# A graph-attention layer and an expert layer in one kernel: the first group's look-ups, the split of src and the tables of pairs take other places in the order

## The chip, the cores and the metric

The kernel runs on one core of one Trainium2 chip. The metric is the device time of one execution in microseconds (us). A core has five engines that work side by side and hand over by semaphores: TensorE (PE, matrix products and transposes), VectorE (DVE), ScalarE (ACT), GpSimd (POOL) and SyncE (SP, which here only issues transfers). Each engine takes its own instructions strictly in the order in which the program lists them, so an instruction that waits holds up all that stand behind it on its engine.

## What is computed

```python
xn  = layernorm(x)                                   # x: 6250 x 256
xt  = (xn @ weight).reshape(6250, 4, 64)
row, col = src, dst                                  # only the first 6250 edges reach the output
a   = softmax(leaky_relu(al(xt[row]) + ar(xt[col])), axis=heads)   # al, ar: products with attn_l, attn_r
tmp = sum over heads of a[n, h] * xt[col[n], h, :]
x   = x + tmp, the same 64 columns for each of the 4 heads
t   = layernorm(x)
logits = t @ router_w.T;  top 2 of 8 experts, two weights
x   = x + t + sum over the two experts of weight * (gelu(t @ w1[e] + b1[e]) @ w2[e] + b2[e])
```

## The kernel before

Rows lie on 128 partitions in 49 tiles; five groups of 10, 10, 9, 10 and 10 tiles are worked one after the other. The order on every engine is the order of the program text (manual schedule): no planner moves anything. The first 190 us or so have these stages.

**Setup (lines 186 to 365).** SP issues the loads of dst, src and x, ACT those of the weights. PE, DVE and ACT fold the weights (`raw`, `own`, `terms`, `turned`, `twice`). Lines 337 to 358 are the split of src on DVE: eleven small instructions turn each index into a partition number `hi` and a column `low`. Line 360 transposes `hi` on PE into the PSUM tile `pe`, line 362 copies it to `high_b` on DVE, and lines 364 and 365 send it through DRAM back to all partitions as `high_1`.

**The source phase (lines 679 to 696).** Thirteen blocks `k` of up to four tiles of x. For each, PE transposes the *next* block (`turn`, line 247), then multiplies this one (`own_terms`, line 434); ACT copies the result to `own_T` (line 439), and PE turns it back one block later (`back`, line 448). Beside this DVE computes the row statistics of each of four parts (`source_statistics`, lines 418 and 420) and ends each part (`source_end`, lines 457 to 467), which yields `al_sb`. The dictionary `fillers` hangs other work on single blocks: `weights_columns` behind block 1, `pair_tables` behind block 2, the tables `low_0` (line 664) and `high_1` (line 667) behind blocks 7 and 8. In `weights_columns` PE makes two PSUM tiles `pv` (line 372), and DVE copies both into `w_sb` (line 376).

**Gathers (lines 235 and 655 to 659).** `paced` is a tiny copy on POOL (`pace`), which waits for a given tile, followed by two indirect transfers that fetch rows of x by dst. From block 3 on each block's `own_T` paces two gathers; later each second tile of the features paces two more. So 20 gathers hang on the source phase and ten more on the tiles of the first group, and all stand on POOL's queue ahead of `feature_root(0)` (lines 470 to 472), which makes `rstd_d` of the first group.

**Features (lines 768 to 792).** For each tile PE multiplies the gathered, transposed rows by `w_sb` (`px`, line 480); ACT copies the product (line 488) and takes the row's mean square (line 490). After each second tile `look_up` (lines 509 and 513) picks out al of the source rows by eight matmuls over `high_1`, `al_sb`, `huge_b` and `low_0` into the PSUM tile `pl`; DVE reduces it later (line 517, held in `pending`). In the second tile of a group DVE begins the attention of the group before (`attend_1`, line 524, which needs `rstd_d`), then ACT takes the exponents (line 538), and so on up to the routing (`route`), whose last result `mine_all` (line 610) PE needs for `rank` (line 622).

**Experts (from line 1167).** After a global sort of the rows by expert pair, 125 units of products, bound by PE.

PSUM tiles come from one pool `ps` with two buffers for each tag, handed out in turn: a third tile of a tag gets the first one's buffer and must wait until that has been read. Tag `px` is used by `pm` (line 288), by the two `pv`, and then by the features; `pe` has tag `r`.

Of the kernel before, what the change touches and what calls it, by code (L numbers as in the profile page):

```python
# [9 lines left out]
FP = mybir.dt.float32  # L10
BF = mybir.dt.bfloat16
I32 = mybir.dt.int32
AF = mybir.ActivationFunctionType
ALU = mybir.AluOpType
# [8 lines left out]
def kernel(  # L23
# [37 lines left out]
    nc = tc.nc  # L61
    N, D = x.shape
    H, OC = attn_l.shape
    NE, _, F = w1.shape
    P = 128
    NT = -(-N // P)
# [3 lines left out]
    GROUPS = [(0, 10), (10, 10), (20, 9), (29, 10), (39, 10)]  # L70
# [13 lines left out]
    NPAIR = len(PATH)  # L84
# [17 lines left out]
    HUGE = 2.0**127  # L102
# [7 lines left out]
    ps = ctx.enter_context(tc.tile_pool(name="ps", bufs=2, space=PSUM))  # L110
    dram = ctx.enter_context(tc.tile_pool(name="dram", bufs=1, space=DRAM))
    ctx.enter_context(tc.manual_schedule())

    def wide(v, n):
        return v.rearrange("p (t k) -> p t k", k=1).to_broadcast([v.shape[0], v.shape[1], n])
# [16 lines left out]
    ident = const.tile([128, 128], FP, name="ident")  # L132
# [13 lines left out]
    huge_b = held.tile([128, 128], BF, name="huge_b")  # L146
# [16 lines left out]
    high_1 = held.tile([P, NTE * P], BF, name="high_1")  # L163
# [15 lines left out]
    small = early.enter_context(tc.tile_pool(name="small", bufs=2))  # L179
# [6 lines left out]
    first_pool = setup.enter_context(tc.tile_pool(name="setup", bufs=1))  # L186
# [3 lines left out]
    src_sb = first_pool.tile([P, NT], I32, name="src_sb")  # L190
# [118 lines left out]
    for k in range(H // 2):  # L309
# [2 lines left out]
            pf[:, NE:].rearrange("p (s h) -> p s h", h=H)[:, :, 2 * k : 2 * k + 2],  # L312
        )

    def heads(c):
        return w_sb[:, c, :AR].rearrange("p (h k) -> p h k", k=HB)

# [15 lines left out]
        nc.vector.tensor_copy(own[:, c, :H], pa[:, 1, :])  # L333
        nc.vector.tensor_copy(w_sb[:, c, AR:MEAN], pa[:, 0, :])


    src_f = first_pool.tile([P, NT], FP, name="src_f")
    nc.vector.tensor_copy(src_f, src_sb)
    nc.vector.tensor_scalar(src_sb, src_sb, 4, None, ALU.logical_shift_right)
    nc.vector.tensor_scalar(src_sb, src_sb, 171, None, ALU.mult)  # L340
    nc.vector.tensor_scalar(src_sb, src_sb, 9, None, ALU.logical_shift_right)
    hi = first_pool.tile([P, NT], FP, name="hi")
    nc.vector.tensor_copy(hi, src_sb)
    lo = first_pool.tile([P, NT], FP, name="lo")
    nc.vector.scalar_tensor_tensor(
        lo, hi, -float(PER), src_f, op0=ALU.mult, op1=ALU.add
# [9 lines left out]
    )  # L356
    nc.vector.tensor_tensor(src_f, src_f, over, ALU.mult)
    nc.vector.tensor_tensor(hi, hi, src_f, ALU.add)
    pe = ps.tile([NT, P], FP, name="pe", tag="r")
    nc.tensor.transpose(pe, hi, ident)  # L360
    high_b = first_pool.tile([NT, P], BF, name="high_b")
    nc.vector.tensor_copy(high_b, pe)
    highs = dram.tile([1, NT * P], BF, name="highs")
    nc.sync.dma_start(highs.rearrange("o (t p) -> (o t) p", p=P), high_b)
    nc.sync.dma_start(high_1[:, : NT * P], highs.to_broadcast([P, NT * P]))

    def weights_columns():

# [13 lines left out]
    def pair_tables():  # L382

        nc.vector.tensor_scalar(before_b, count_up, number, None, ALU.is_gt)
        nc.vector.tensor_scalar(huge_b, ident, -HUGE, None, ALU.mult)
        nc.vector.tensor_scalar(valid, number, float(LAST), None, ALU.is_lt)

        nc.vector.tensor_scalar(
            outside, number, float(LAST), float(2 * NS * TS), ALU.is_ge, ALU.mult
        )  # L390


        for e in range(NE):
            nc.vector.memset(order[:, e : e + 1], 2.0 ** (NE - e))


        one_of = first_pool.tile([P, 2, NPAIR], FP, name="one_of")
        for i, (a, b) in enumerate(PATH):
            for k, e in enumerate((a, b)):
                nc.vector.memset(one_of[:, k, i : i + 1], float(e))  # L400
        for i, (a, b) in enumerate(PATH):
            nc.vector.memset(pairs[:, i : i + 1], 2.0 ** (NE - a) + 2.0 ** (NE - b))

        other = small.tile([NS, NE, NPAIR], FP, name="other", tag="mr", bufs=1)
        for k, to in enumerate((member, other)):
            nc.vector.tensor_tensor(
                to,
                one_of[:NS, k : k + 1, :].to_broadcast([NS, NE, NPAIR]),
                wide(count_up[:NS, :NE], NPAIR),
                ALU.is_equal,  # L410
            )
        nc.vector.tensor_tensor(member, member, other, ALU.add)
# [63 lines left out]
    def features(g, i, blocks, k):  # L476

        px = ps.tile([P, C], FP, name="px", tag="px")
        for c in range(DC):
            nc.tensor.matmul(  # L480
                px, blocks[c][:, k * P : (k + 1) * P], w_sb[:, c, :],
                start=(c == 0), stop=(c == DC - 1),
            )
        if i == 0:
            pxss[g] = work.tile([P, GROUPS[g][1], C], FP, name="pxs")
            sqs[g] = tiny("sq", GROUPS[g][1], 3)
        pxs = pxss[g]
        nc.scalar.copy(pxs[:, i, :], px)  # L488
        junk = work.tile([P, D], FP, name="junk", bufs=1)
        nc.scalar.activation(  # L490
            junk, xd(GROUPS[g][0] + i), AF.Square, bias=pxs[:, i, MEAN:], scale=ROOT_D,
            accum_out=sqs[g][:, i : i + 1],
        )

    def feature_root(g):
        rstd_ds[g] = tiny("rstd_d", GROUPS[g][1], 3)
        root(rstd_ds[g], sqs.pop(g))
# [3 lines left out]
    def look_up(g, i, n):  # L501

        if i == 0:
            ags[g] = small.tile([P, GROUPS[g][1], H], FP, name="ag", tag="ag")
        pl = ps.tile([P, n, H, NT], FP, name="pl", tag="m")
        for k in range(n):
            t = GROUPS[g][0] + i + k
            for part in range(3):
                nc.tensor.matmul(  # L509
                    pl[:, k, :, :], high_1[:, t * P : (t + 1) * P],  # L510
                    al_sb[:, part, :, :], start=(part == 0), stop=False,
                )
            nc.tensor.matmul(  # L513
                pl[:, k, :, :], huge_b,
                low_0[:, t : t + 1, :].to_broadcast([P, H, NT]), start=False, stop=True,
            )
        return lambda: nc.vector.tensor_reduce(ags[g][:, i : i + n, :], pl, AX.X, ALU.max)  # L517
# [137 lines left out]
    def paced(t, n, of):  # L655

        nc.gpsimd.tensor_copy(pace[: of.shape[0]], of)
        for i in range(t, min(t + n, NT)):
            gather(i)

    fillers = {
        1: weights_columns,
        2: pair_tables,
        7: lambda: nc.vector.tensor_tensor(
            low_0[:, :NT, :], long(count_up[:, :NT], NT), wide(low, NT), ALU.not_equal
        ),
# [8 lines left out]
    def turn_features(k):  # L675
        g, b, n = FEATURES[k]
        return turn(xd, GROUPS[g][0] + b, n)
# [54 lines left out]
    pending = []  # L732

    def settle():
        while pending:
            pending.pop(0)()

    def tasks(g):

        n = GROUPS[g][1]  # L740
        at = {i: [] for i in range(n)}

        def put(i, what):
            at[min(i, n - 1)].append(what)

        if g >= 1:
            f = g - 1
            m = GROUPS[f][1]
            put(1, lambda: attend_1(f))
            put(2, lambda: exponents(f))  # L750
            put(2, lambda: attend_2(f))
            for i in range(0, m, 3):
                put(3 + i // 3, lambda i=i: attend_3(f, i, min(3, m - i)))
            steps = route(f)
            for i in range(5):
                put(7 + i // 2, lambda: next(steps))
        if g >= 2:
            f2 = g - 2
            put(1, lambda: rank(f2))
            put(2, lambda: ranked(f2))  # L760
        if g == 3:
            put(0, load_experts)
        if g == 4:
            put(0, load_biases)
        return at

    at = {}
    for k, (g, b, n) in enumerate(FEATURES):
        if b == 0:
            at = tasks(g)  # L770
        after = None
        for j in range(n):
            i = b + j
            features(g, i, blocks, j)
            t = GROUPS[g][0] + i
            if t % 2 == 0 and t + AHEAD < NT:
                paced(t + AHEAD, 2, pxss[g][:, i, :1])
            if j == 0 and k + 1 < len(FEATURES):
                after = turn_features(k + 1)
            settle()  # L780
            if i % 2:
                pending.append(look_up(g, i - 1, 2))
            elif i == GROUPS[g][1] - 1:
                pending.append(look_up(g, i, 1))
            if i == GROUPS[g][1] - 1:
                feature_root(g)
                if g == 2:
                    counting()
            for what in at[i]:
                what()  # L790
        blocks = after
    settle()


# [431 lines left out]
```

## Time and profile before

| what | value |
|---|---|
| median of 3 runs | 432.43 us (431.76 to 432.58) |
| the profiled execution | 430.84 us, of which its span from first to last instruction is 429.1 us |
| mean granted TensorE clock | 0.926 of full |
| busy over the span | PE 368.8 us, DVE 312.5 us, ACT 226.0 us, POOL 199.9 us |
| 192 to 320 us (experts) | PE busy all of the 128.00 us |
| 75 to 150 us (features) | PE busy 54.67 us, DVE 64.44 us |
| 43 to 54 us | PE busy 5.89 of 11.00 us at a granted clock of 0.69 |

The 40 digits of the page's second part are the span in equal slices of 10.7 us; the waits name an engine, what it wanted to do and what released it, with the total, the number and the longest in us; the timeline gives start, duration, engine, line, operation, output and input, count, and in brackets the idle time ahead of it with its releaser.

### The profile page before, as it was taken

How to read it: one execution, taken by the hardware profiler on the slowest of the kernel's cores; microseconds unless marked ns; L12 is line 12 of the kernel's file. 1: busy time of each engine (PE TensorE's matmuls, PEld its weight loads, DVE VectorE, ACT ScalarE, POOL GpSimd, SP SyncE). 2: the span in 40 equal slices, each digit the busy share in tenths (PEclk: the TensorE clock that was granted, in tenths of full speed). 3: DMA queues.
4: the chain of work that ended last, by engine and by line, in shares of the span. 5: the costliest groups of instructions: out<-in, count | busy, mean ns of one | idle time of the engine just before them, and what ended most of it. 6: DMA issues, size and time to landing. Idle time of an engine off the chain costs nothing.

```text
span 429.1 us, 9886 instructions
## 1 busy us (share of the span) xinstructions
PE 368.8 (86%) x2575; PEld 320.0 (75%) x2575; DVE 312.5 (73%) x1092; ACT 226.0 (53%) x658; POOL 199.9 (47%) x240
## 2 busy tenths in 40 slices
PE   5798599888992127979999999999999999999990
PEld 4676388777881115469999999999998899999990
DVE  5999525897988896548778778877876877555551
ACT  3486279575762000057666666667665666333330
POOL 0068888888202000573343567667656633233222
PEclk9699699999997555799999999999999999999997
DMA  7974232446663110766667677777777765666610
GB/s 218 354 236 135 74 105 73 162 168 191 210 227 162 80 80 0 215 185 164 196 178 197 188 233 219 212 224 235 216 217 196 202 192 180 190 186 186 177 69 23
DMA packets 53896, 74.63 MB, mean 174 GB/s; under 512 B 7686, under 2 KB 48250, under 8 KB 52948
## 3 DMA queue, kind: packets, MB, share of 16 engines
q1 hardware_dynamic: 46028, 52.45, 39.9%
q0 software_dynamic: 7248, 21.29, 16.6%
q8 instruction: 23, 0.38, 0.4%
q10 hardware_dynamic: 568, 0.27, 0.3%
q14 instruction: 29, 0.24, 0.2%
HBM read 59.13 MB, written 14.87 MB: 172 GB/s over the span
## 4 chain that ended last, share of the span: by engine, by line
PE 49%; POOL 2%; issue 2%; ACT 1%; DVE 1%; POOLq 0%; ACTq 0%; DVEq 0%
PE ph L1117 24%; PE py L1133 23%; PE pt L1063 2%; POOL xr L939 1%; POOL nm L1020 1%; ACT hid L1124 0%; POOLq L1221 0%; DVE acc L1140 0%; DVE stats L1014 0%; ACT tok L1030 0%; ACTq L1077 0%; ACT acc L1040 0%; POOL out_dram L1144 0%; ACT tokT L1064 0%; POOL mv L1019 0%
## 5 line engine op out<-in xcount | busy, mean ns | idle before, releaser
L1117 PEld LDWEIGHTS ph<-tokT,w 128*128 128x128 f32 x1000 | 130.2, 191 | 13.8 <-ACT tokT L1064 7.7
L1117 PE MATMUL ph<-tokT,w 128*128 (+1 forms) x1000 | 132.5, 276 | 4.8 <-ACT tokT L1064 4.6
L1133 PE MATMUL py<-big,hid 128*128 x500 | 128.6, 380 | 0.0
L1124 ACT ACTIVATE hid<-ph,b_cols 128x128 f32<-128x128 f32 x250 | 77.9, 363 | 75.4 <-PE ph L1117 74.2
L1133 PEld LDWEIGHTS py<-big,hid 128*128 128x128 f32 x500 | 85.4, 191 | 7.0 <-DVE acc L1140 0.2
L939 POOL DMA_INDIRECT xr<-table,held_by x49 | 49.6, 1013 | 72.7 <-DVE held_by L913 39.2
L1140 DVE SCALAR_TENSOR_TENSOR acc<-py,shares,acc 128x256 f32 (+1 forms) x125 | 60.5, 484 | 28.0 <-PE py L1133 17.3
L1144 POOL DMA_INDIRECT out_dram<-acc,held_out x49 | 50.9, 1038 | 55.4 <-DVE acc L1140 39.2
L1140 DVE SCALAR_TENSOR_TENSOR acc<-big,shares,acc (+1 forms) x125 | 60.2, 481 | 11.3 <-issue 6.1
L1030 ACT ACTIVATE tok<-xr,nm 128x256 f32<-128x256 f32 x49 | 29.3, 599 | 60.9 <-DMA w<-in_L_ffn_w_dram 42.2
L480 PE MATMUL px<-w_sb,tT 128*128 128x293 f32 x196 | 56.6, 420 | 0.0
L480 PEld LDWEIGHTS px<-w_sb,tT 128*128 128x128 f32 x196 | 35.0, 194 | 7.3 <-issue 0.3
L236 POOL DMA_INDIRECT big<-in_x_dram,dst_sb x31 | 34.3, 1107 | 7.2 <-issue 6.8
L488 ACT COPY pxs<-px 128x293 f32<-128x293 f32 x49 | 19.8, 404 | 27.6 <-PE px L480 25.3
L251 ACT COPY tT<-pt 128x512 f32<-128x512 f32 (+2 forms) x56 | 26.9, 527 | 9.3 <-PE pt L247 8.9
L1004 DVE TENSOR_TENSOR xr<-xr 128x512 f32<-128x512 f32 (+1 forms) x25 | 17.2, 688 | 17.0 <-issue 17.0
L1040 ACT ACTIVATE acc<-xr,nm 128x256 f32<-128x256 f32 x49 | 29.1, 597 | 0.0
L509 PE MATMUL pl<-al_sb,high 128*128 128x196 bf16 x147 | 19.4, 250 | 8.0 <-DVE al_sb L464 5.9
L509 PEld LDWEIGHTS <-high 128*128 128x128 bf16 x147 | 13.6, 98 | 13.8 <-issue 6.1
L517 DVE TENSOR_REDUCE ag<-pl 128x8 f32<-128x392 f32 (+1 forms) x25 | 13.8, 551 | 11.8 <-PE pl L513 11.8
L1019 POOL TENSOR_SCALAR mv<-mv 128x2 f32<-128x2 f32 (+1 forms) x25 | 5.7, 229 | 35.0 <-DVE mv L1016 33.3
L236 POOL DMA_INDIRECT xd_own<-in_x_dram,dst_sb x18 | 18.5, 1027 | 4.4 <-issue 2.7
(217 smaller groups left out, 478.2 us busy)
## 6 DMA issues: line engine op xcount, KB each, us to landing
w<-in_L_ffn_w_dram SPq DMA_DIRECT2D x125, 256.0 KB
table<-x SPq DMA_DIRECT2D x4, 1685.0 KB
x<-in_x_dram SPq DMA_DIRECT2D x10, 512.0 KB
big<-in_L_ffn_w_dram SPq DMA_DIRECT2D x2, 1024.0 KB
high<-highs SPq DMA_DIRECT2D x1, 1568.0 KB
table<-x SPq DMA_DIRECT2D x1, 1516.5 KB
big<-in_L_ffn_b_dram SPq DMA_DIRECT2D x1, 1024.0 KB
xr<-table,held_by POOLq DMA_INDIRECT x49
```

Of the source, the lines that this page charges most:

```text
L236: nc.gpsimd.indirect_dma_start(out=xd(t), out_offset=None, in_=x[:, :], in_offset=bass.IndirectOffsetOnAxis(ap=dst_sb[:, t : t + 1], axis=0),)
L251: nc.scalar.copy(tT, pt)
L480: nc.tensor.matmul(px, blocks[c][:, k * P : (k + 1) * P], w_sb[:, c, :], start=(c == 0), stop=(c == DC - 1),)
L509: nc.tensor.matmul(pl[:, k, :, :], high_1[:, t * P : (t + 1) * P], al_sb[:, part, :, :], start=(part == 0), stop=False,)
L939: nc.gpsimd.indirect_dma_start(out=xr[:, i, :], out_offset=None, in_=table[:, :], in_offset=bass.IndirectOffsetOnAxis(ap=held_by[:, s0 + i ...
L1030: nc.scalar.activation(tok[:, i, :], xr[:, i, :D], AF.Identity, bias=bias[:, i : i + 1], scale=scale[:, i : i + 1],)
L1040: nc.scalar.activation(acc[:, s * D : (s + 1) * D], xr[:, i, :D], AF.Identity, bias=bias[:, i : i + 1], scale=more[:, i : i + 1],)
L1117: nc.tensor.matmul(ph[:, j, :], w[:, c * F + j * 128 : c * F + (j + 1) * 128], tokT[:, bass.ds(rows_at + c * TS, TS)], start=(c == 0), sto ...
L1124: nc.scalar.activation(hid[:, j, :], ph[:, j, :], AF.Gelu, bias=b1_cols[:, :, j][:, bass.ds(at_act[u][0], 1)])
L1133: nc.tensor.matmul(py, hid[:, j, :], we2[:, j, bass.ds(at_pe[u][1], D)], start=(j == 0), stop=(j == FC - 1),)
L1140: nc.vector.scalar_tensor_tensor(to, y, share, to, op0=ALU.mult, op1=ALU.add)
L1144: nc.gpsimd.indirect_dma_start(out=ends_at[s][:, :], out_offset=bass.IndirectOffsetOnAxis(ap=held_out[:n, s : s + 1], axis=0), in_=acc[:n, ...
```

## The change

Four things are moved, and the arithmetic stays the same.

- The first five instructions on src (up to the first `hi`) stand ahead of the copies of `pa` into `own` and `w_sb` on DVE; the other six stay.
- The transpose of `hi`, the copy `high_b` and the two transfers become a function `sources`, a filler behind block 2. Its PSUM tile `pe` takes tag `px` in place of `r`.
- `pair_tables` leaves the source phase; it is called in the features of the first group, behind tile 3. `huge_b` is taken out of it and becomes a filler behind block 6. `one_of` lies in another pool.
- Look-ups go through a list `waiting`. In the first group none is issued before tile 7; behind tiles 7 and 8 two each are issued, behind tile 9 the last. The other groups keep their places.

```diff
+    src_f = first_pool.tile([P, NT], FP, name="src_f")
+    nc.vector.tensor_copy(src_f, src_sb)
+    nc.vector.tensor_scalar(src_sb, src_sb, 4, None, ALU.logical_shift_right)
+    nc.vector.tensor_scalar(src_sb, src_sb, 171, None, ALU.mult)
+    nc.vector.tensor_scalar(src_sb, src_sb, 9, None, ALU.logical_shift_right)
+    hi = first_pool.tile([P, NT], FP, name="hi")
+    nc.vector.tensor_copy(hi, src_sb)
...
         nc.vector.tensor_copy(own[:, c, :H], pa[:, 1, :])
         nc.vector.tensor_copy(w_sb[:, c, AR:MEAN], pa[:, 0, :])
-    src_f = first_pool.tile([P, NT], FP, name="src_f")
-    nc.vector.tensor_copy(src_f, src_sb)
-    nc.vector.tensor_scalar(src_sb, src_sb, 4, None, ALU.logical_shift_right)
-    nc.vector.tensor_scalar(src_sb, src_sb, 171, None, ALU.mult)
-    nc.vector.tensor_scalar(src_sb, src_sb, 9, None, ALU.logical_shift_right)
-    hi = first_pool.tile([P, NT], FP, name="hi")
-    nc.vector.tensor_copy(hi, src_sb)
...
-    pe = ps.tile([NT, P], FP, name="pe", tag="r")
-    nc.tensor.transpose(pe, hi, ident)
-    high_b = first_pool.tile([NT, P], BF, name="high_b")
-    nc.vector.tensor_copy(high_b, pe)
-    highs = dram.tile([1, NT * P], BF, name="highs")
-    nc.sync.dma_start(highs.rearrange("o (t p) -> (o t) p", p=P), high_b)
-    nc.sync.dma_start(high_1[:, : NT * P], highs.to_broadcast([P, NT * P]))
+    def sources():
+        pe = ps.tile([NT, P], FP, name="pe", tag="px")
+        nc.tensor.transpose(pe, hi, ident)
+        high_b = first_pool.tile([NT, P], BF, name="high_b")
+        nc.vector.tensor_copy(high_b, pe)
+        highs = dram.tile([1, NT * P], BF, name="highs")
+        nc.sync.dma_start(highs.rearrange("o (t p) -> (o t) p", p=P), high_b)
+        nc.sync.dma_start(high_1[:, : NT * P], highs.to_broadcast([P, NT * P]))
...
     def pair_tables():
         nc.vector.tensor_scalar(before_b, count_up, number, None, ALU.is_gt)
-        nc.vector.tensor_scalar(huge_b, ident, -HUGE, None, ALU.mult)
...
-        one_of = first_pool.tile([P, 2, NPAIR], FP, name="one_of")
+        one_of = small.tile([P, 2, NPAIR], FP, name="one_of", bufs=1)
...
     fillers = {
         1: weights_columns,
-        2: pair_tables,
+        6: lambda: nc.vector.tensor_scalar(huge_b, ident, -HUGE, None, ALU.mult),
+        2: sources,
...
+    waiting = []
...
             settle()
-            if i % 2:
-                pending.append(look_up(g, i - 1, 2))
-            elif i == GROUPS[g][1] - 1:
-                pending.append(look_up(g, i, 1))
-            if i == GROUPS[g][1] - 1:
+            last = i == GROUPS[g][1] - 1
+            if i % 2 or last:
+                waiting.append((g, i - i % 2, 1 + i % 2))
+
+            for _ in range(0 if g == 0 and i < 7 else 2 if len(waiting) > 1 else 1):
+                if waiting:
+                    settle()
+                    pending.append(look_up(*waiting.pop(0)))
+            if g == 0 and i == 3:
+                pair_tables()
+            if last:
                 feature_root(g)
```

More of the change, by code (lines that the diff above doesn't have):

```diff
@@ L791 @@
         blocks = after
+    assert not waiting
     settle()
```

## The prediction

> **What bounds the kernel now.** I read the page first: from 192 us on PE is never idle for long, and the change touches nothing there, so what counts is when the stages ahead of it end. Then the waits of the first 75 us:
>
> ```profile
> POOL pace L657 <- ACT own_T L439: 21.9, 1, 21.9
> ...
> PE pl L509 <- DVE al_sb L464: 5.9, 3, 5.6
> ...
> DVE z L524 <- POOL rstd_d L472: 4.8, 1, 4.8
> ...
> PE pe L360 <- DVE hi L358: 2.5, 1, 2.5
> ```
>
> PE loses 5.6 us ahead of the first look-up and 2.5 us ahead of `pe`. But DVE, which those look-ups feed, then waits 4.8 us for POOL. So the third view is POOL's timeline:
>
> ```profile
> 23.05 0.18 POOL L657 COPY pace<-own_T 128x1 f32<-128x1 f32 x1 [21.87 <-ACT own_T L439]
> 23.41 1.17 POOL L236 DMA_INDIRECT xd_own<-in_x_dram,dst_sb  x1 [0.18 <-DMA x<-in_x_dram]
> ...
> 25.87 0.18 POOL L657 COPY pace<-own_T 128x1 f32<-128x1 f32 x1
> ...
> 28.97 0.19 POOL L657 COPY pace<-own_T 128x1 f32<-128x1 f32 x1
> ...
> 40.91 4.25 POOL L236 DMA_INDIRECT big<-in_x_dram,dst_sb  x1 [0.31 <-issue]
> ...
> 65.84 0.28 POOL L471 TENSOR_SCALAR sq<-sq 128x10 f32<-128x10 f32 x1
> 66.21 2.00 POOL L472 TENSOR_TENSOR rstd_d<-sq,minus_half 128x10 f32<-128x10 f32 x1
> ```
>
> From 23.05 us, when `own_T` of block 3 frees the first pace, POOL has no idle time but issue gaps: 15 pairs of gathers (a pair takes 2.58 us undisturbed), then `rstd_d`. Not one pace waits again. The stall of PE at 42 us left no mark here. `rstd_d` of the first group comes at 68.21, 45.16 us after the first pace, whatever PE does meanwhile. DVE's timeline shows who waits:
>
> ```profile
> 13.63 4.00 DVE L418 BATCH_NORM_STATS2 stats<-x 128x6 f32<-128x256 f32 x12
> ...
> 23.21 0.27 DVE L376 COPY w_sb<-pv 128x32 f32<-128x32 f32 x2
> ...
> 68.24 0.20 DVE L524 TENSOR_TENSOR z<-pxs,rstd_d 128x40 f32<-128x40 f32 x1 [4.76 <-POOL rstd_d L472]
> ...
> 85.40 0.20 DVE L524 TENSOR_TENSOR z<-pxs,rstd_d 128x40 f32<-128x40 f32 x1 [1.42 <-POOL rstd_d L472]
> ```
>
> At the second group DVE waits for POOL once more (1.42), and from there DVE is nearly full to the routing at 148 us. So the path is: first pace, POOL's queue, `rstd_d`, DVE. What moves the end is the moment of `own_T` of block 3.
>
> **Part 1, the split of src.** The five instructions took 10.61 to 11.68. They go into DVE's idle 1.57 us ahead of line 333 (8.44 to 10.01), if src has landed; line 345 then starts behind the last copy of line 334 at 10.68 instead of 11.71: 1.03 gained. Its last transfers were issued on ACT at 5.37 to 6.16. One near row: SP's second x load waited for the small attn transfer issued at 1.88 and went at 5.32, so some 3.2 us; src then lands at about 9.2 (estimate), early enough. Bounds: 8.44 (gain 1.03) and 10.61, where DVE waited for nothing (gain below nothing by the four copies of `own`, about 0.3). From this place `high_b` and its wait also go (12.88 to 13.63, 0.75), 1.78 together. So the statistics of part 0 start at 13.63 - 1.78 = 11.85, or at 13.25 by the other end. I take 11.85.
>
> **Part 2, `pe` behind block 2.** PE gains its 2.52 us at first. From 13.18 (turn of block 1) to 21.05 it did all that now stands ahead of `pe`, 7.87 us, and so from 10.42 on it reaches `pe` at 18.3, or near 16.5 if the half clock of 10.8 to 17.6 goes. But `pe` is now the fourth tile of tag `px`, behind `pm` and two `pv`, so it gets the buffer of the first `pv`, which line 376 must have read. On DVE that copy stands behind the statistics of parts 0 and 1. It was at 23.21; with its first half (0.14) and 0.06 hand-over, less 1.78, PE goes on at T = 21.65 (upper end 23.05). PE idles 3.4 to 5.1 us, and behind `pe` stand the turn of block 4, `own_terms` of block 3 and so `own_T` of block 3, on which POOL hangs.
>
> From the turn of block 4 (21.05) to the first pace (23.05) took 2.00 us at full clock: with 0.2 for `pe`, the pace is at T + 2.2 = 23.85, 0.8 late. At half clock the same stretch is block 1's turn to block 0's `own_T` (13.18 to 16.17), 2.99 + 0.27 + 0.06: T + 3.55 = 25.2, 2.15 late. Which clock? The windows:
>
> ```profile
> 10.84:14.25 3.41, 1.31 (x7) 1.31 (x7) 2.63 (x13) 0.00 (x0) 0.00 (x0) 0.50 1.08 359
> 14.25:17.67 3.42, 3.42 (x28) 2.58 (x27) 3.42 (x13) 1.86 (x4) 0.00 (x0) 0.52 1.09 356
> ...
> 41.56:44.97 3.41, 0.69 (x3) 0.19 (x1) 3.41 (x3) 2.30 (x7) 3.41 (x1) 0.98 0.06 22
> 44.97:48.38 3.41, 0.42 (x2) 0.30 (x3) 2.89 (x15) 0.00 (x0) 2.80 (x6) 0.50 0.27 77
> ```
>
> The first number after the length is PE's busy time, the third from the end the granted clock. PE stopped at 42.25 and the clock was halved 2.7 us later; it stopped at 10.42 and the clock was halved within 0.5 us, and stayed so until 17.6 though PE worked again from 12.94. The Trainium skill (TensorE: Matmul & The Clock Gate, Part 1) says that the clock halves after at least one idle window of about 3.4 us. By that rule a gap of 3.4 to 5.1 us only sometimes holds a whole window, and the sum would use 0.8; by the rows 0.4 to 2.7 us were enough, and it uses 2.15. I take the rows. The second pace hangs on block 4, also at half clock and behind ACT's table load of 1.28 us: 0.2 more.
>
> SP: the two transfers of `highs` stood behind the x loads (issued until 20.5); now SP waits for `high_b` at about 22.4, with nothing behind but the `table` writes at 83 us. `high_1` was asked for at 26.44 and used at 43.2; asked for at 28.6 at the latest, with 8 us of traffic as before (26 to 34 us), it is there by 37: nothing. If that cover were gone, the wait would fall on DVE's line 667.
>
> **Part 3, `pair_tables`.** Its 3.4 us (23.41 to 27.20 less `huge_b` and a gap) leave DVE, yet DVE gains nothing: `source_end(0)` needs ACT's `std`, which stands behind `own_T` of block 3 and the table load, T + 5.05 = 26.7 against 27.20 before. `al_sb` is so complete near 48.7, as before. In its new place it fills DVE from 48.7 to 52.2, which was idle but for single reductions of 0.56; `huge_b` costs 0.22 there. The Trainium skill speaks against this place: GpSimd shares its SBUF interfaces with DVE and contends with instructions of two SBUF inputs (GPSIMD Engine Reference, 1. Specifications). The row agrees: the gather under lines 664 and 667 took 4.25 us for 0.95. The tables hold only three such instructions (0.38 each), and POOL gathers at both places; the pair under them took 3.10 for 2.58. So 0.5 leaves and returns: nothing, bounds -0.5 and +0.5. The 3.3 under lines 664 and 667 stay.
>
> **Part 4, the late look-ups.** PE reaches tile 7's look-ups near 52 (end of tile 1, 42.25 + 2.35, and 7.2 of products); `al_sb` is there, so the 5.55 stall and the half clock behind it go. Worth to the end: nothing, since PE then waits for POOL's `rstd_d` instead: ACT stands at the exponents of group 0 and PE behind it at tile 5 of the second group, from about 66.7 to 72.4. That gap halves the clock again. Before, PE needed 12.3 us from that tile to `rank` and waited 0.87 for `mine_all`; with some 2.5 lost to the clock it comes up to 1.3 late, which ACT's next exponents pass to DVE. Bounds 0 and 1.3; I take 0.5, as DVE has 1.42 of slack there. ACT's second table load now lies in the wait: -0.25.
>
> **Sum.** 2.15 + 0.2 + 0.5 - 0.25 = +2.6. The profiled execution's 430.84 becomes 433.4. It lay 1.6 below the median of 432.43, so I expect 435.0.
>
> **The rivals.**
> (a) Faster: the buffer is free when PE comes. Place: `pe` at 18.3. Then `own_T` of block 3 ends 2.9 earlier and POOL's whole queue with it: 429.5. It decides where `pe` goes before 20.85 at full clock or 19.5 at half. For it: DVE's start may move more than I see. Against: the copy of `pv` stands behind 9.8 us of statistics that start at 11.85 at the earliest. 10%.
> (b) The change does what it seems to: the 5.55 stall and some 2.2 of half clock come off the end, 424.7. Against: the 4.76 that DVE waits for POOL. 3%.
> (c) As forecast, but at full clock, so +0.8 + 0.1 (second pace) - 0.25 + 0.3: 433.4. 20%.
> (d) As forecast, with src late (+1.4) or PE's whole 1.3 in the second group: 436.4. 17%.
> The forecast itself: 50%.
>
> **The numbers.** A difference of 0.2%, 0.86 us, is about what a measurement can tell from none. Faster is (a) and (b), 13%; of (c) half lies within, with 2% of the forecast's lower tail: same 12%; the rest, 75%, slower. The range from 432.3 to 436.8 leaves out (a) and (b) and the top of (d).
>
> **What would show it.** Right: `pe` on PE waits for line 378 (the copy of `pv`) until about 21.7; the first pace on POOL at about 25.2; `rstd_d` near 70.5; no stall at the first look-up, but PE idle near 67 to 72. Wrong: `pe` without a wait, or a first pace before 23.05; POOL idle between the first pace and `rstd_d`, or DVE at line 524 without a wait for it, since then POOL is not the bound.

## The result, and the profile after

| | before | after |
|---|---|---|
| median of 20 runs | 432.62 us (431.08 to 434.61) | 434.12 us (433.02 to 435.32) |
| ratio, 95% interval | | 1.0032 (1.0019 to 1.0045) |
| the profiled execution, its span | 430.84, 429.1 us | 433.76, 432.0 us |

The change makes the kernel slower by 0.3%, 1.5 us by the medians. The two profiled executions lie 2.9 us apart, because that of before lies 1.8 below its median and that of after only 0.4. In all tables here a median counts every run, while a ratio leaves out the few executions that took over 1.5% more than the fastest of their kernel (two of before, two of e10 and one of e12, all in the third set below).

I read the same views as before, in the same order. First the waits of the first 75 us (engine, what it wanted, what released it: total, number, longest):

```profile
POOL pace L658 <- ACT own_T L440: 23.8, 2, 23.4
DVE z L525 <- POOL rstd_d L473: 12.9, 1, 12.9
...
PE px L481 <- ACT pxs L489: 7.5, 1, 7.5
...
DVE rstd L458 <- ACT std L456: 3.3, 1, 3.3
...
PE pe L362 <- DVE w_sb L378: 2.5, 1, 2.5
```

The wait of 5.6 us that PE had at the first look-up is gone. In its place PE waits 7.5 us later on, and DVE waits 12.9 us instead of 4.8 for POOL's `rstd_d`: the early stall was exchanged for a late one. At `pe` the 2.5 us are the same as before, but now the releaser is DVE's copy of `pv`, not `hi`. PE's timeline has both places:

```profile
22.24 0.31 PE L362 MATMUL pe<-ident,hi 128*49 128x128 f32 x1 [2.52 <-DVE w_sb L378]
...
71.90 2.32 PE L481 MATMUL px<-w_sb,tT 128*128 128x293 f32 x4 [7.54 <-ACT pxs L489]
```

POOL's timeline, from the first pace to `rstd_d` of the second group:

```profile
24.61 0.18 POOL L658 COPY pace<-own_T 128x1 f32<-128x1 f32 x1 [23.43 <-ACT own_T L440]
...
27.74 0.18 POOL L658 COPY pace<-own_T 128x1 f32<-128x1 f32 x1 [0.32 <-ACT own_T L440]
...
40.05 4.33 POOL L236 DMA_INDIRECT big<-in_x_dram,dst_sb  x1 [0.30 <-issue]
...
68.13 1.99 POOL L473 TENSOR_TENSOR rstd_d<-sq,minus_half 128x10 f32<-128x10 f32 x1
...
72.85 0.84 POOL L658 COPY pace<-pxs 128x1 f32<-128x1 f32 x1
...
86.12 2.00 POOL L473 TENSOR_TENSOR rstd_d<-sq,minus_half 128x10 f32<-128x10 f32 x1
```

The first pace is 1.56 late (23.05 before), the second 1.87 (25.87), `rstd_d` of the first group starts 1.92 late, that of the second 2.97 (83.15). No pace waits after the second one. DVE's timeline shows where the first lateness is made and where it goes:

```profile
12.44 4.01 DVE L419 BATCH_NORM_STATS2 stats<-x 128x6 f32<-128x256 f32 x12
17.29 4.01 DVE L419 BATCH_NORM_STATS2 stats<-x 128x6 f32<-128x256 f32 x12
22.03 0.27 DVE L378 COPY w_sb<-pv 128x32 f32<-128x32 f32 x2
...
70.15 0.20 DVE L525 TENSOR_TENSOR z<-pxs,rstd_d 128x40 f32<-128x40 f32 x1 [12.88 <-POOL rstd_d L473]
...
88.16 0.20 DVE L525 TENSOR_TENSOR z<-pxs,rstd_d 128x40 f32<-128x40 f32 x1 [2.78 <-POOL rstd_d L473]
```

Two blocks of statistics stand ahead of the copy that `pe` needs, and DVE has no gap there. At the other end DVE begins the attention of the first two groups the moment `rstd_d` is there, 1.91 and 2.76 later than before (68.24 and 85.40). At the third group it begins without a wait, at 104.02 against 101.34, so 2.68 late, and the span ends 2.9 late.

### The profile page after: what moved, and what is told of

Read it like the earlier page. It is cut to its first block, busy times and chain, and to the rows that moved or that the text cites. A ratio compares the mean times of both kernels' runs of the same rounds, so it can differ in the third digit from the quotient of the medians.

```text
span 432.0 us, 9885 instructions
## 1 busy us (share of the span) xinstructions
PE 371.8 (86%) x2575; PEld 322.5 (75%) x2575; DVE 312.0 (72%) x1092; ACT 226.6 (52%) x658; POOL 202.2 (47%) x240
## 4 chain that ended last, share of the span: by engine, by line
PE 43%; DVE 4%; POOL 3%; issue 3%; ACT 1%; DVEq 1%; POOLq 0%; ACTq 0%
PE ph L1127 21%; PE py L1143 20%; DVE acc L1150 2%; PE pt L1073 2%; POOL xr L949 1%; POOL nm L1030 1%; DVEq L1087 1%; DVE stats L1024 1%; ACT hid L1134 0%; POOLq L1231 0%; POOL mv L1029 0%; POOL out_dram L1154 0%; ACTq L1087 0%; ACT acc L1050 0%; ACT tokT L1074 0%
## 5 line engine op out<-in xcount | busy, mean ns | idle before, releaser
L236 POOL DMA_INDIRECT big<-in_x_dram,dst_sb x31 | 35.2, 1137 | 7.2 <-issue 6.8
L1030 POOL TENSOR_TENSOR nm<-mv,half_c 128x2 f32<-128x2 f32 (+1 forms) x25 | 18.3, 733 | 2.1
```

The source lines that it names most:

```text
L236: nc.gpsimd.indirect_dma_start(out=xd(t), out_offset=None, in_=x[:, :], in_offset=bass.IndirectOffsetOnAxis(ap=dst_sb[:, t : t + 1], axis=0),)
```

## The experiments

Four kernels were run together three times, each time on another chip and beside the kernel before, whose median was 432.42, 432.44 and 444.01 us: e1 to e4, e5 to e8, e9 to e12. The third time all kernels took longer, so those four are compared by their ratio alone. All four profiles of this third set show one thing that none of the other ten shows: in the tables of pairs DVE's tiny `MEMSET`s have gaps of about 0.65 us between them. No kernel before was profiled there. Two landmarks are given from each kernel's own profile: the first pace on POOL, and the start of the first group's attention on DVE (line 524 or 525), which starts when both `rstd_d` and the look-up are there.

| kernel | median us | ratio (95%) | first pace | attention | span | span less attention |
|---|---|---|---|---|---|---|
| before | 432.62 | 1 | 23.05 | 68.24 | 429.1 | 360.9 |
| after | 434.12 | 1.0032 (1.0019 to 1.0045) | 24.61 | 70.15 | 432.0 | 361.9 |
| e1_pv_on_act | 428.60 | 0.9903 (0.9881 to 0.9925) | 21.35 | 66.20 | 427.3 | 361.1 |
| e2_pe_behind_block3 | 430.60 | 0.9960 (0.9945 to 0.9975) | 21.41 | 66.82 | 428.5 | 361.7 |
| e3_early_lookups | 434.39 | 1.0043 (1.0030 to 1.0056) | 26.92 | 71.63 | 432.9 | 361.3 |
| e4_only_pe_moved | 435.19 | 1.0068 (1.0044 to 1.0092) | 26.12 | 71.12 | 433.1 | 362.0 |
| e5_only_late_lookups | 431.90 | 0.9994 (0.9977 to 1.0010) | 22.98 | 68.07 | 429.6 | 361.5 |
| e6_before_ahead14 | 432.03 | 1.0002 (0.9987 to 1.0018) | 23.59 | 66.92 | 430.2 | 363.3 |
| e7_after_ahead14 | 426.71 | 0.9878 (0.9854 to 0.9902) | 24.95 | 62.02 | 424.1 | 362.1 |
| e8_after_pe3_ahead14 | 422.77 | 0.9785 (0.9755 to 0.9815) | 20.90 | 59.00 | 421.2 | 362.2 |
| e9_late_and_ahead14 | 436.34 | 0.9858 (0.9813 to 0.9904) | 23.11 | 67.59 | 432.1 | 364.5 |
| e10_pv_act_ahead14 | 435.06 | 0.9832 (0.9775 to 0.9888) | 18.77 | 61.93 | 427.6 | 365.7 |
| e11_pe_in_old_place | 443.30 | 1.0017 (0.9989 to 1.0044) | 22.34 | 76.86 | 442.3 | 365.4 |
| e12_pv_act_ahead10 | 442.57 | 0.9992 (0.9956 to 1.0028) | 21.41 | 64.65 | 438.4 | 373.8 |

The last column is the reading on which the others rest: among the ten profiles before e9 the attention moves by 12.6 us, and what follows it stays between 360.9 and 363.3.

**Was it the wait for the buffer?** e1_pv_on_act is the changed kernel, but ACT frees the buffer:

```diff
-            nc.vector.tensor_copy(heads(c)[:, :, OC : OC + NE], pv)
+            nc.scalar.copy(heads(c)[:, :, OC : OC + NE], pv)
```

> The changed kernel with one edit: ACT instead of DVE copies the two pv into w_sb, so that pe's buffer is free before PE reaches it. Theory (the path is first pace, POOL's queue, rstd_d): pe on PE at about 19.6 us without a wait, the first pace on POOL at about 21.9 (24.61 in the changed kernel), rstd_d of the first group at about 67.4 (70.12), and the time 2.7 less than the changed kernel: about 431.4. Rival 1 (POOL's queue does not carry: the 2.8 between the traces comes from elsewhere): pace earlier, but time within 0.5 of the changed kernel, 434. Rival 2 (the half clock, not the buffer, makes the pace late): first pace still at 23.5 or later, and about 433.

PE's timeline, and then POOL's:

```profile
19.23 0.27 PE L362 MATMUL pe<-ident,hi 128*49 128x128 f32 x1
```

```profile
21.35 0.18 POOL L658 COPY pace<-own_T 128x1 f32<-128x1 f32 x1 [20.16 <-ACT own_T L440]
```

`pe` runs without a wait, 3.0 earlier than in the changed kernel, the pace comes 3.3 earlier, the attention 3.95, the span ends 4.7 earlier. The time fell by 5.5 against the median after, twice what I expected; 428.6 is also below the kernel before. The theory's mechanism holds and both rivals fall. Most of the size is in the profile: with the gap the half clock behind it goes, so the pace gains 0.25 more than `pe`; the second pace no longer waits its 0.32; and what POOL loses under the two big tables of DVE (lines 666 and 669) is 3.05 us, not 3.38 (a pace of 1.78 and a gather of 2.41 for 0.19 and 0.95; in the profile after, a gather of 4.33 for 0.95). These make 3.26 + 0.32 + 0.33 = 3.91 of the 3.95 up to the attention. Behind it, 0.8 more lies within the spread of the table's last column, and the rest of the 5.5 stays open. So the change was worth something, and it was undone by the place of `pe` in the order of one PSUM tag. Which of its moves brings how much of that gain was not separated, and the kernel before was not run with ACT's copies alone.

**Or a later place?** e2_pe_behind_block3 moves `sources` behind block 3:

```diff
-        2: sources,
...
+        if k == 3:
+            sources()
```

> The changed kernel with sources moved one block later, behind the gathers and products of block 3, so that own_T of block 3 no longer stands behind pe; the wait for the buffer itself may stay. Theory: first pace at about 22 us (24.61), rstd_d of the first group at about 67.5, time about 431.4. If instead only the total idle time of PE counts, the wait moves behind block 3 and the time stays at 434. If it is the second pace that counts (own_T of block 4 behind the wait), some 0.5 us of the gain is lost: 431.9.

First pace 21.41; PE still waits 1.31 us for the buffer, and the second pace 0.46 for `own_T` of block 4 (24.66 us). The time is 430.6, 3.5 below the changed kernel and 0.8 below the first expectation: what cost was that `own_T` of block 3 stood behind `pe`. PE's wait also shrank, from 2.52 to 1.31, and the clock stayed at full behind it, but it ends at 22.32, when the first pace is already past.

**Part 2 alone.** e4_only_pe_moved is the kernel before with `sources` behind block 2, tag `px`, and nothing else:

```diff
-        2: pair_tables,
+        2: lambda: (sources(), pair_tables()),
```

> The kernel before with one part of the change: pe with its copy and its two transfers becomes a function called behind block 2 (ahead of pair_tables), its PSUM tile takes tag px. Theory: pe waits for DVE's copy of pv, the first pace comes some 1.5 to 2.3 us later than before (23.05), rstd_d of the first group as much later than 68.21, and the time is 1.5 to 2 more than the kernel before: about 434.3. Rival (the time of the change comes from the late look-ups or from pair_tables): within 0.5 of the kernel before, 432.6.

PE's timeline, and then POOL's:

```profile
22.55 0.45 PE L361 MATMUL pe<-ident,hi 128*49 128x128 f32 x1 [4.71 <-DVE w_sb L377]
```

```profile
26.12 0.31 POOL L658 COPY pace<-own_T 128x1 f32<-128x1 f32 x1 [24.94 <-ACT own_T L440]
```

PE waits for the copy of `pv` until 22.55, the first pace is 3.07 late and the time 2.8 more than before. The mechanism is as expected, the size beyond what I gave (1.5 to 2.3 and 1.5 to 2): PE's gap is longer than in the changed kernel, and the pace comes 3.57 behind `pe` at half clock, 2.37 in the profile after. Part 2 alone is thus enough for the whole slowdown.

**Late look-ups.** e5_only_late_lookups adds them alone to the kernel before, e3_early_lookups takes them alone out of the changed one. The edit of e3 (e5 is the other way round):

```diff
-                waiting.append((g, i - i % 2, 1 + i % 2))
-
-            for _ in range(0 if g == 0 and i < 7 else 2 if len(waiting) > 1 else 1):
-                if waiting:
-                    settle()
-                    pending.append(look_up(*waiting.pop(0)))
+                pending.append(look_up(g, i - i % 2, 1 + i % 2))
```

> The kernel before with only the late look-ups: none in the first group before tile 7, two behind tile 7 and tile 8, one behind tile 9. Theory: PE's wait of 5.6 us for al_sb goes, but PE then waits longer ahead of the second group, since rstd_d of the first group still comes near 68.2; time within 0.5 of the kernel before, 432.6. Rival (b of the prediction): the stall and its half clock come off the end, 7.7 us less: 425. Rival (the half clock in the second group reaches the end): 0.5 to 1.3 more, 433.5.

> The changed kernel with the look-ups of the first group issued as before the change, behind each second tile; the rest of the change stays. Theory (the stall of PE at the first look-up is covered by POOL's rstd_d): PE waits some 5 us for al_sb near 43 us again, PE's wait of 7.5 us near 64 to 72 us shrinks by as much, rstd_d at 70.1 as in the changed kernel; time within 0.6 of the changed kernel, 434.1. Rival (the late look-ups save PE's stall and its half clock on the path, rival b of the prediction): slower than the changed kernel by 5 to 8 us. Second rival (PE's idle time ahead of the second group costs clock and delays it): faster by 0.5 to 0.9 us.

Both give nothing, 431.90 and 434.39. DVE's timeline of e5 tells why:

```profile
68.07 0.20 DVE L524 TENSOR_TENSOR z<-pxs,rstd_d 128x40 f32<-128x40 f32 x1 [12.38 <-POOL rstd_d L472]
```

DVE gets ready 7.8 us earlier than before and waits 12.38 instead of 4.76, to start at the same time. e3 shows something else as well. Its DVE code up to here is that of the changed kernel, yet its timeline reads:

```profile
11.31 0.19 DVE L317 CAST src_f<-src_sb 128x49 f32<-128x49 int32 x1 [2.56 <-issue]
...
13.65 4.01 DVE L419 BATCH_NORM_STATS2 stats<-x 128x6 f32<-128x256 f32 x12
```

In the profile after, `src_f` stood at 8.65 without a wait. Over the profiles with the split of src it came at 8.65, 9.24, 9.26, 9.40, 9.51, 9.58, 9.69, 10.30 and 11.31, six times with the load of src named as releaser: src often lands after DVE wants it. (In e3 and e7 no releaser is seen; that src is the cause there too is inferred.) In e3 the wait pushed the statistics to 13.65 (1.21 later than in the profile after), the copy of `pv` to 23.24 and the first pace to 26.92; the other 1.10 of the pace's 2.31 is the clock, which here was at half almost from `pe` on. So part 1 put a load with uncertain landing ahead of the path; in the five profiles with the old place, at 10.43 to 11.16, DVE did not wait for it.

**POOL's queue.** e6_before_ahead14 and e7_after_ahead14 take three pairs of gathers out of the queue ahead of `rstd_d`, in the kernel before and in the changed one:

```diff
-    AHEAD = 20
-    OWN_FROM = len(OWN) - AHEAD // 2
+    AHEAD = 14
+    OWN_FROM = 3
...
-        if k >= OWN_FROM:
+        if OWN_FROM <= k < OWN_FROM + AHEAD // 2:
```

> The kernel before with 14 instead of 20 gathers hung on the source phase (blocks 3 to 9), so that 24 instead of 30 stand on POOL's queue ahead of rstd_d of the first group. Theory (POOL's queue is the bound): rstd_d comes earlier by three pairs of 2.58 us, as far as the features give it its input: the squares of tile 9 at about 63.3 us, so rstd_d ends near 65.7 instead of 68.21, and the time falls by 2 to 3 us: about 430. PE or DVE then binds. Rival (POOL does not bind, PE's stall at the first look-up does): no change, 432.6. Rival (gathers come too late for the later tiles): slower by over 2 us.

> The changed kernel with 14 instead of 20 gathers hung on the source phase. Theory: here PE has no stall at the first look-up, so the features' squares of the first group come near 56 us, and rstd_d of the first group comes some 7 to 8 us earlier than 70.12, near 62.5; DVE's wait of 12.9 us for it nearly goes; the time falls by as much as the stages behind can use: 426 to 429. The late look-ups are then worth something: e7 should be 2 us or more below the same edit of the kernel before. Rival (POOL's queue is not what the late look-ups ran into): time within 1 us of the changed kernel.

In the kernel before: nothing (1.0002), a miss of mine. DVE's timeline of e6:

```profile
66.92 0.20 DVE L524 TENSOR_TENSOR z<-pxs,rstd_d 128x40 f32<-128x40 f32 x1 [2.76 <-ACT pxs L488]
...
70.78 0.20 DVE L545 TENSOR_REDUCE s<-ex 128x10 f32<-128x40 f32 x1 [2.25 <-ACT ex L538]
```

The attention starts 1.32 earlier, now released by ACT and no longer by POOL, and then DVE waits 2.25 for the exponents, which stand on ACT behind the products of the second group. The sum of the exponents comes at 70.78 against 70.10 before. PE still has its stall at the first look-up in e6 (5.48 us, until 47.93), and its lateness arrives here. It even reaches POOL, since the later gathers are paced by the products: at 52.59 a pace waits 4.73 us for `pxs`. So in the kernel before two things end within a microsecond of each other: POOL's queue, and PE's stall by way of ACT. Each hides the other.

In the changed kernel, where the stall is gone, the same edit brings 7.4 us. DVE's timeline of e7, whose attention stood at 70.15 without the edit:

```profile
62.02 0.20 DVE L525 TENSOR_TENSOR z<-pxs,rstd_d 128x40 f32<-128x40 f32 x1 [4.97 <-POOL rstd_d L473]
```

Within one set e5 and e6 have 0.9994 and 1.0002, and e7, with both of their edits and the rest of the change, 0.9878: this already speaks for two chains that hide each other.

e9_late_and_ahead14 is the clean form of this, the kernel before with the two edits that alone brought nothing:

> The kernel before with two edits together that alone gave nothing: the late look-ups (alone 0.9994 of the kernel before) and 14 gathers in the source phase (alone 1.0002). Theory (at the first attention POOL's rstd_d and the pair of PE and ACT, held up by the stall at the first look-up, arrive within a us of each other, so that each hides the other): together rstd_d of the first group ends near 59.5 to 60.5 us (68.21 before) and the time falls by 6 to 8, to about 425.5. Rival (the two add up): within 0.6 of the kernel before, 432.4, and then the gain of 7.4 in the changed kernel with 14 gathers comes from its other parts.

Ratio 0.9858 (0.9813 to 0.9904), some 6 us: they do not add up, they need each other. (The two single edits were not run again in this third set.) The landmark of 60 us was missed by 7; in that profile POOL waited for its paces several times more (1.74 us at 36.57, 1.39 at 43.46, 1.76 at 62.25). With no profile of the kernel before from this set, where the 6 us are won can't be read.

**The best version.** e8_after_pe3_ahead14 joins e2 and e7, e10_pv_act_ahead14 joins e1 and e7, e12_pv_act_ahead10 goes on to ten gathers (`AHEAD = 10`):

> The changed kernel with sources behind block 3 and 14 gathers hung on the source phase: both bounds of the change taken away. Theory: first pace near 22 us, rstd_d of the first group near 60; the time 0.5 to 2.7 below that of the changed kernel with 14 gathers alone, as PE or DVE may bind there instead: 424 to 428. Rival: equal to that kernel, since POOL no longer binds.

> The changed kernel with ACT's copies of pv and 14 gathers in the source phase: pe without a wait and a shorter queue. Theory: the two add up, since both act on the same queue: first pace near 21.4, rstd_d of the first group ending near 58.2, time 362 more than that by the profile: about 421.5. Rival (DVE or PE binds behind 59 us): no better than the variant with sources behind block 3 and 14 gathers, 422.8 or more.

> The changed kernel with ACT's copies of pv and only 10 gathers in the source phase, 20 ahead of rstd_d of the first group. Theory: two more pairs of 2.58 leave the queue, but DVE waited only some 4.8 for rstd_d with 14 gathers, and the squares of tile 9 come next, so at most 4.8 off: 417 to 421. Rival (what is not fetched ahead is late for its tile: PE waits for gathered rows): 422 to 426.

e8 is the fastest, 422.77, 2.15% below the kernel before, and 3.9 below e7. The parts add up: e2 took 3.5 off the changed kernel, e7 took 7.4, and e8 takes 11.4. e10 gave 0.9832 from four executions between 429.34 and 435.40, which would be 425.2 at the first sets' level, and its interval (0.9775 to 0.9888) reaches to e8: which of the two is better stays open, the more so as the tables of pairs held DVE up in e10. e12 lost all of it against e10, whose tables were as slow. Its waits from 75 to 130 us:

```profile
PE pt L247 <- DMA xd_own<-in_x_dram,dst_sb: 6.5, 4, 2.9
```

PE waits for gathered rows, and the attention of the fourth group starts at 121.91 (113.59 in e10): what is not fetched ahead comes late there, as the rival said, at more cost than its 422 to 426.

**Part 2 undone.** e11_pe_in_old_place is the changed kernel with the seven lines of `sources` back in their old place and `pe` with tag `r`.

> The changed kernel with part 2 undone: pe, high_b and the two transfers in their old place and with tag r; the split of src, the tables and the look-ups as in the change. Theory (part 2 alone makes the change slower): pe waits for hi only, about 1 us shorter than the 2.5 before; first pace between 22.0 and 23.05, rstd_d of the first group ending between 67 and 68.4; time 431 to 432.6, not slower than the kernel before. Rival (the tables of pairs or the late look-ups cost in their new places): 433.5 or more.

Its ratio, 1.0017 (0.9989 to 1.0044), does not decide between the two. `pe` waited 1.40 us for `hi` and the first pace came at 22.34, as the theory has it, but `rstd_d` ended at 76.83, not between 67 and 68.4: POOL's paces waited for the products (`pxs`), once 3.37 us until 61.07. DVE's timeline shows what goes with it:

```profile
49.78 0.17 DVE L400 MEMSET one_of<- 128x1 f32 x10
50.41 0.06 DVE L400 MEMSET one_of<- 128x1 f32 x1 [0.46 <-issue]
51.12 0.08 DVE L400 MEMSET one_of<- 128x1 f32 x2 [0.65 <-issue]
```

The tables of pairs took from 49.3 to 61.7, with such gaps between the `MEMSET`s, while in the profile after all 56 of them took 1.08. e10 and e12 have the same, and e9 a little of it in the old place behind block 2 (two gaps, 0.60 and 0.63). What holds them up, no profile here shows. So e11 is no test of part 2; that part 2 is the cause rests on e1, e2 and e4.

## Why the prediction was right, and where its terms were off

The mechanism was right: first pace, POOL's queue, `rstd_d`, DVE; `pe` behind the copy of `pv`; no stall at the first look-up and PE idle before the second group instead (0.46 us busy from 64 to 72). Term by term, by the profile after:

- **Part 1, statistics from 11.85:** measured 12.44. src had landed (8.65), as estimated, but the products `pa` reached DVE only at 10.37 and 11.22, so the four copies of line 342 and 343 had gaps of 0.65 and 0.62, which I had not put in. In other executions the loss was src itself (the bound of 13.25, passed in e3 with 13.65).
- **Part 2, `pe` at 21.65:** measured 22.24, later by just what the statistics were later. From the start of the statistics to the copy of `pv` it is 9.59 in each of the six profiles in which `pe` waits for this copy (after, e2, e3, e4, e7, e8), so this step was sound. PE came to it at 19.72, not 18.3, since it worked at half speed until nearly 17 us. PE's timeline after, the same sixteen products for block 0 and for block 2:

```profile
12.91 1.08 PE L435 MATMUL pa<-tT,own 128*32 128x128 f32 x16
...
18.82 0.64 PE L435 MATMUL pa<-tT,own 128*32 128x128 f32 x16
```

  In e7 they took 0.64 from block 0 on, and PE came at 16.53. The granted clock in the windows reads 1.00 in both, so it shows nothing of this slow beginning.
- **First pace, T + 3.55 = 25.2:** measured 24.61, T + 2.37. The terms that the sum names (2.99, 0.27, 0.06) make 3.32; it needs the 0.33 from `own_T` to the pace as well (22.72 to 23.05 before), so 3.55 stands. The clock did fall, but too late to act on all of the stretch. The windows of the profile after (PE's busy time behind the length, granted clock third from the end):

```profile
22.00:23.00 1.00, 0.76 (x7) 0.77 (x8) 0.59 (x7) 0.00 (x0) 0.00 (x0) 1.00 0.97 290
23.00:24.00 1.00, 1.00 (x20) 0.61 (x18) 0.00 (x0) 0.92 (x2) 0.00 (x0) 0.81 0.38 102
24.00:25.00 1.00, 1.00 (x10) 0.83 (x5) 0.00 (x0) 0.85 (x3) 0.21 (x2) 0.50 0.09 31
```

  In e3, e4 and e7 the same stretch took 3.47, 3.57 and 3.56, the forecast's half clock. Which of the two it is depends on where the gap falls; in e7 PE stopped at 16.5 and the clock was halved before 19 us, long before `pe` came. The value I took was that of three executions of four. One of its two rows was misread, though: in e4 the clock also fell to half at 10.7 us (0.64 in 10.5 to 11.0, 0.50 in the next half us), and there PE was at work from 9.24 to 17.85. So the fall at 10.7 in the kernel before can hardly be laid to the gap that had just begun at 10.42, and it does not follow that 0.4 us of a gap are enough. That the clock fell at all behind a gap of 2.52, where 3.4 to 5.1 were forecast, was in part luck.
- **Second pace, 0.2:** measured 0.31.
- **Second group, +0.5 for the clock and -0.25 for the table load:** measured +0.85 from the first to the second attention (18.01 against 17.16), and the term was put in the wrong place. POOL carries it: it is never idle from 68.13 to 86.12 but for issue gaps, its five pairs took 15.65 us against 14.62 before, with single gathers of 1.29 to 1.61 and a pace of 0.84 beside DVE's line 557 and 562. That DVE's instructions stretch them is argued from this, not tested. Nor does it belong to the late look-ups: e3 and e4, with early ones, have 17.79 and 17.72. The 17.16 of the profile before is the exception.
- **Part 3, nothing:** as the prediction has it, DVE waited 3.33 for ACT's `std` (at 26.20; 26.7 forecast), and `al_sb` was there for the late look-ups. That holds for the profile after; in e11 the tables took 12.4 us instead of 3.4.
- **The sum:** +2.6 forecast, +2.9 between the two profiles, +1.5 between the medians. What is left is the base: the prediction set its 2.6 on top of the median, but took the rows it compared with from an execution 1.8 below that median. Its short second group (17.16, where the profiles of e1 to e5 have 17.71 to 17.79) is one thing that seems not to be there in an ordinary execution; the rest is not located.

Rival (a), the free buffer, came true in no profile of the changed order; e1 makes the buffer free by an edit, and it gave 428.6 where (a) had 429.5 (its own 18.3 and 2.2 give a pace 2.55 earlier, not 2.9). Rival (b) fell with e5. But the sentence that the stall at the first look-up left no mark was too strong. It held with the long queue; e6 and e9 show that the stall was worth about 6 us as soon as POOL's queue was short.

## What to carry to other kernels

When a tile is moved in the program, find out which earlier tile of its tag must have been read, on which engine, and what stands ahead of that read: here one small copy behind 10 us of statistics made the change a loss, and giving the copy to another engine made it a gain. Where removing a stall brings nothing, look for a second chain that ends at the same moment and test the two together: two edits of 0.9994 and 1.0002 made 0.9858. A late load and the clock moved the first pace by 2.3 us between two profiles of the same code up to there (24.61 after, 26.92 in e3), and PE's slow beginning moved it by 2.6 between two others (18.77 in e10, 21.41 in e12). That is more than the change moved the time, so compare landmarks over several profiles before a term is believed.

## What the runs showed of the hardware

- The clock of PE: gaps of 1.31 (e2) and 1.80 us (e8) left the eight transposes behind them at 1.04 us, PE's full speed. Gaps of 2.52 (after), 3.68 (e3), 4.71 (e4) and 4.86 us (e7) each went with a fall to half; in the profile after it came nearly 4 us past the moment PE stopped, when PE had been at work again for more than a microsecond. The Trainium skill (TensorE: Matmul & The Clock Gate, Part 1) speaks of at least one idle window of about 3.4 us, which runs free of the program. The free-running part fits the spread; a whole idle window of that length is not there in a gap of 2.52 us. Nor is a gap always needed: in e4 the clock fell at 10.7 us with PE at work, and why stays open.
- The granted clock in the windows says nothing before its first change: it reads 1.00 in the profile after while PE took 1.08 us for products that it did in 0.64 later. Go by the durations of like instructions there.
- The landing of one small load varied: DVE could start on src between 8.65 and 11.31 us in nine profiles with the same order of transfers (between 9.26 and 10.30 in the six in which src is named as the releaser).
- An indirect gather on POOL that lay under the two tables of lines 666 and 669 took 4.33 us in the profile after and 4.15 in e2, against 0.95 alone; in e1 a pace of 1.78 and a gather of 2.41 shared the same stretch.
